# A perceiver block on one core: where the attentions of the tokens keep their row sums and largest scores in PSUM

## The chip, the core and the metric

The kernel runs on one core of a Trainium2 chip. The metric is the device time of one execution in microseconds (us); the median of several runs is compared. The profile shown here is one further execution, taken with the hardware profiler. TensorE is called PE (its weight loads PEld), VectorE DVE, ScalarE ACT, GpSimd POOL and SyncE SP.

## The reference

Twelve blocks are added to x one after another, x being 2 sequences of 256 tokens with 256 features: four times a cross attention, a self attention and a feed-forward part. The edit touches the self attentions of the second and the fourth layer (L1 and L3), both with 16 heads of 16 features. That of L1, shortened to what matters:

```python
scale = jnp.asarray(k, x.dtype) ** 0.25
q = (jnp.einsum('btk,ok->bto', x, Wq) / scale).reshape(b, t, H, hd)
kk = (jnp.einsum('btk,ok->bto', x, Wk) / scale).reshape(b, t, H, hd)
v = jnp.einsum('btk,ok->bto', x, Wv).reshape(b, t, H, hd)
dot = jnp.einsum('bthd,bshd->bhts', q, kk)
att = jax.nn.softmax(dot, axis=-1)
out = jnp.einsum('bhts,bshd->bthd', att, v).reshape(b, t, k)
return jnp.einsum('btk,ok->bto', out, Wu) + bu
```

That of L3 is the same with biases and with a band: a query sees the keys that are at most 128 tokens away. In front of each attention is a layer norm.

## The kernel before

Both attentions are the class SmallAttention (L1336), called by small_attention (L1322). The 16 heads lie in four chunks c of four heads, each head in 32 of the 128 partitions; 2 sequences b by 4 chunks are the 8 units (b, c), u = 0 to 7, of `UNITS` (L1342). A unit has 256 queries and 256 keys for four heads.

For one unit the work is a chain:

- **first_scores** (L1451): PE makes the scores with the queries in the partitions (`both`, matmuls at L1430, groups s<-sa_k,sa_q of two pairs of heads; L3 adds the band with matmuls at L1438), and DVE takes the largest of each row, negated, from each pair (L1455), into sa_top.
- **shift_queries** (L1463): PE transposes the largest scores into a bank of PSUM, top_ps (L1467), and DVE adds them to a spare row of the queries (L1468), so that the second scores come out with the largest already taken off.
- **scores** (L1470): PE makes the scores again with the keys in the partitions (L1430, s<-sa_q,sa_k, in L3 with L1438), and ACT takes the exponential of each pair (L1475), into p.
- **weigh** (L1478): PE multiplies p with the values (L1485) into attn_acc; one more column of the values is 1, so that the sums of the weights come out beside the result. ACT copies the accumulator into a (L1493).
- **Net.inverses** (L195): PE turns the rows with the sums into columns (sums, matmul at L180), and DVE takes their reciprocals (L201).
- **Net.to_heads** and **normalize** (L204, L1495): PE spreads the reciprocals over each head's partitions (den, L209) and DVE multiplies a by them into sa_oT (L1500).

The loop `attend` (L1405) runs as a pipeline of n + 4 = 12 steps. In step i it calls inverses for unit i-4, shift_queries for i-1, first_scores for i, weigh for i-3, scores for i-1 and normalize for i-4. PE, DVE and ACT run in the order in which the program issues (`manual_schedule`, L1325), so this order is the order of each engine's queue; no planner is in it. No DMA is issued in the loop.

All of PSUM's eight banks are in use in the loop (L1330): `banks(mm=1, sc=3, acc=1)`, that is three pairs of banks for scores (tag sc), one bank for the accumulator (acc), one for everything else (mm). sums, top_ps and den are each a whole new bank with the tag mm, so each of the three waits until the reader of the one before it is done. The queries of the next unit use the same three sc pairs in turn: a step takes four of them.

The same inverses and to_heads also serve the cross attentions of L0 and L1 (the class ContextAttention, L780), with banks of their own.

Of the kernel before, what the change touches and what calls it, by code (L numbers as in the profile page):

```python
# [28 lines left out]
S = 256  # L29
# [41 lines left out]
class Net:  # L71
# [120 lines left out]
            nc.vector.tensor_tensor(rest, of, part, ALU.subtract)  # L192
        nc.vector.tensor_copy(outs[:, 2, ..., :n], rest)

    def inverses(self, a):  # L195

        ps = self.mm("sums")
        for qt in range(2):
            self.matmuls(ps[:, qt * NG : (qt + 1) * NG], [(a[:, qt * P : (qt + 1) * P], self.den)])
        r = self.small.tile([P, 2, NG], F32, tag="inverses", name="inverses", bufs=2)  # L200
        self.nc.vector.reciprocal(r, ps[:, : 2 * NG].rearrange("p (q g) -> p q g", g=NG))  # L201
        return r

    def to_heads(self, r):  # L204

        ps = self.mm("den")
        for qt in range(2):
            for g in range(NG):
                self.nc.tensor.matmul(  # L209
                    ps[g * HP : (g + 1) * HP, qt * P : (qt + 1) * P],  # L210
                    lhsT=r[:, qt, g : g + 1].to_broadcast([P, HP]),
                    rhs=self.ident,
                    start=True,
                    stop=True,
                )
        return ps[:, :S]
# [105 lines left out]
    def self_attention(self, work, qT, kT, v_of, oT, mask=None, causal=False, gates=None, before=None, negated=None):  # L322
# [98 lines left out]
        with self.tc.manual_schedule(engines=by_program):  # L421
            if before is not None:
                before(0)
            for n in range(len(items) + 6):
                if before is not None and n % 4 == 1 and n // 4 + 1 < qT.shape[1]:
                    before(n // 4 + 1)
                if n < len(items):
                    scores(n)
                if 0 <= n - 1 < len(items):
                    share(n - 1)  # L430
                if 0 <= n - 3 < len(items):
                    transpose(n - 3)
                if 0 <= n - 5 < len(items) and items[n - 5][2] == 1:
                    weigh(n - 5)
# [153 lines left out]
def run(steps, n=None):  # L588

    for _ in steps if n is None else zip(range(n), steps):  # L590
        pass


class Focus:
# [28 lines left out]
    def weigh(self, y, total, factor):  # L623


        nc = self.nc
        top, norm = (self.net.sm(NT, name=n, tag=n) for n in ("f_top", "f_norm"))
        nc.scalar.activation(y, y, AF.Ln, bias=self.eps)

        ready = self.net.sm(1, name="ready", tag="ready")  # L630
        nc.scalar.activation(ready, self.eps, AF.Exp)
        nc.gpsimd.tensor_scalar(y, y, self.power[:, 0:1], 1.0, ALU.mult, ALU.mult)
        yield
        nc.vector.tensor_reduce(top, y, AX.X, ALU.max, negate=True)
        yield
        for t in range(NT):
            nc.scalar.activation(
                y[:, t, :], y[:, t, :], AF.Exp, bias=top[:, t : t + 1], accum_out=norm[:, t : t + 1]
            )
            if t % 2:  # L640
                yield
        nc.vector.tensor_tensor(factor, total[:, 0, :], total[:, 1, :], ALU.add)
        nc.vector.tensor_scalar(factor, factor, 1.0 / D, 1e-6, ALU.mult, ALU.add)
        nc.vector.reciprocal(norm, norm)
        nc.vector.tensor_tensor(factor, factor, norm, ALU.mult)
# [134 lines left out]
class ContextAttention:  # L780
# [195 lines left out]
    def attend(self, vpool, ppool, fpool):  # L976
        net, nc, PER, LAG = self.net, self.nc, self.PER, self.LAG
        focus = net.focus
        self.vpool, self.ppool = vpool, ppool
        for _ in range(4):  # L980
            self.load_values_ctx()
        focus.start(self.layer, fpool)
        fills = self.plan()
        n = len(self.UNITS)

        ready = net.sm(1, name="ready", tag="ready")
        nc.scalar.activation(ready, net.eps5, AF.Exp)
        rankings = {}
        for g in range((n + 1) * PER + LAG + 2):
            second = g - PER - LAG  # L990
            if g < n * PER:
                self.first_scores(g // PER, g % PER)
            run(self.beginning)
            run(fills.get(g, ()))
            for kc in self.rankings.get(g, ()):
                if kc not in rankings:
                    y, _, factor = focus.chunks[kc]
                    rankings[kc] = focus.sparsify(fpool, y, factor)
                run(rankings[kc], 1)
            if 0 <= second < n * PER:  # L1000
                self.scores(second // PER, second % PER)
            focus.magnitudes_of_taken()
            if 0 <= second - 1 < n * PER:
                self.weigh((second - 1) // PER, (second - 1) % PER)
            if g in self.done:
                self.inverses = net.inverses(self.weighed)
                if self.done[g] == n - 1:
                    run(self.normalize(n - 1))
            for kc in self.weighings.get(g, ()):
                run(focus.weighing[kc], 1)  # L1010
# [73 lines left out]
    def shift_queries(self, u):  # L1084

        nc = self.nc
        ps = self.net.mm("top_ps")
        for qt in range(2):
            nc.tensor.transpose(ps[:, qt * P : (qt + 1) * P], self.tops[qt], self.net.ident)
        yield  # L1090
        nc.vector.tensor_tensor(self.q[u], self.q[u], ps[:, :S], ALU.add)

    def normalize(self, u):

        nc, out = self.nc, self.q[u]
        nc.vector.tensor_tensor(out, self.weighed, self.net.to_heads(self.inverses), ALU.mult)
        if self.v_bias is not None:
            c = self.UNITS[u][1]
            nc.vector.tensor_scalar_add(out, out, self.v_bias[:, c : c + 1])
        yield  # L1100
# [235 lines left out]
class SmallAttention:  # L1336
# [66 lines left out]
            made = []  # L1403

    def attend(self):  # L1405
        n = len(self.UNITS)
        for i in range(n + 4):
            if 0 <= i - 4 < n:
                self.inverses = self.net.inverses(self.weighed[i - 4])
            if 0 <= i - 1 < n:  # L1410
                self.shift_queries(i - 1)
            if i < n:
                self.first_scores(i)
            if 0 <= i - 3 < n:
                self.weigh(i - 3)
            if 0 <= i - 1 < n:
                self.scores(i - 1)
            if 0 <= i - 4 < n:
                self.normalize(i - 4)

    def both(self, name, rows_of, columns_of):

# [37 lines left out]
                negate=True,  # L1460
            )

    def shift_queries(self, u):  # L1463

        ps = self.net.mm("top_ps")
        for qt in range(2):
            self.nc.tensor.transpose(ps[:, qt * P : (qt + 1) * P], self.tops[u % 2][:, qt, :], self.net.ident)  # L1467
        self.nc.vector.tensor_tensor(self.q[u], self.q[u], ps[:, :S], ALU.add)  # L1468
# [9 lines left out]
    def weigh(self, u):  # L1478
        nc = self.nc
        b, c = self.UNITS[u]  # L1480
        acc, ps = self.net.acc("attn_acc"), self.weights.pop(u)
        for kt in range(2):
            for i in range(NG):
                at = (c * NG + i) * VH
                nc.tensor.matmul(  # L1485
                    acc[i * HP : (i + 1) * HP, :S],
                    lhsT=self.v[:, b * 2 + kt, at : at + HP],
                    rhs=ps[i // 2][:, i % 2, kt * S : (kt + 1) * S],
                    start=kt == 0,
                    stop=kt == 1,  # L1490
                )
        self.weighed[u] = self.work.tile([P, S], F32, name="a", tag="a", bufs=3)
        nc.scalar.copy(self.weighed[u], acc[:, :S])  # L1493

    def normalize(self, u):  # L1495

        nc, a = self.nc, self.weighed.pop(u)
        b, c = self.UNITS[u]
        den = self.net.to_heads(self.inverses)
        nc.vector.tensor_tensor(self.oT[:, c, b * S : (b + 1) * S], a, den, ALU.mult)  # L1500


# [825 lines left out]
```

## Time and profile before

| what | us |
|---|---|
| median of the 3 runs | 2512.33 |
| runs | 2512.18, 2512.33, 2951.45 |
| the profiled execution | 2515.34 |
| its span, first to last instruction | 2513.4 |
| L1's attention, from its first scores to its last product | 1644.7 to 1704.3 |
| L3's attention, the same | 2174.5 to 2243.9 |

The mean granted clock of TensorE over the span is 0.958 of full speed. In groups by line, the operations of the loop (both attentions together) are: maxima L1455, 32 of 1221 ns; exponentials L1475, 32 of 1021 ns; L1468 and L1500, 16 each of 421 ns; the copies L1493, 16 of 372 ns. The reciprocals L201 are 32 of 207 ns, of which the cross attentions have half.

In a row of the timeline, the first number is the start in us from the span's start, the second the time from the first start to the last end of a merged group of like instructions; a bracket at the end is the time that the engine was idle before, with what ended it. A matmul of 32-bit numbers, transposes aside, shows as two instructions. A row of the stretches gives the length, then for PE, PEld, DVE, ACT and POOL the busy us with the number of instructions, then TensorE's granted clock, the busy share of the DMA engines and what they moved in GB/s. A row of the waits gives who waited for whom: us in total, times, longest.

### The profile page before, as it was taken

How to read it: one execution, taken by the hardware profiler on the slowest of the kernel's cores; microseconds unless marked ns; L12 is line 12 of the kernel's file. 1: busy time of each engine (PE TensorE's matmuls, PEld its weight loads, DVE VectorE, ACT ScalarE, POOL GpSimd, SP SyncE). 2: the span in 40 equal slices, each digit the busy share in tenths (PEclk: the TensorE clock that was granted, in tenths of full speed). 3: DMA queues.
4: the chain of work that ended last, by engine and by line, in shares of the span. 5: the costliest groups of instructions: out<-in, count | busy, mean ns of one | idle time of the engine just before them, and what ended most of it. 6: DMA issues, size and time to landing. Idle time of an engine off the chain costs nothing.

```text
span 2513.4 us, 42846 instructions
## 1 busy us (share of the span) xinstructions
PE 2336.0 (93%) x17142; PEld 1252.9 (50%) x17142; DVE 1549.4 (62%) x2719; ACT 1093.2 (43%) x1917; POOL 333.2 (13%) x505
## 2 busy tenths in 40 slices
PE   7999999999999689999999999989999996889998
PEld 3455455544544364554454544554448453455454
DVE  4878888788736757877878778443241354334343
ACT  2456555555615333555555565531131252123232
POOL 3000001000024602000010000000011031002120
PEclk9999999999989799999999999989999997798989
DMA  5432232132010133322222220201232100100100
GB/s 185 138 105 86 88 96 94 52 111 64 10 38 35 48 103 108 101 91 90 90 94 86 77 98 28 83 14 43 96 100 93 43 18 14 34 21 12 58 12 21
DMA packets 97798, 174.42 MB, mean 69 GB/s; under 512 B 15120, under 2 KB 63888, under 8 KB 96704
## 3 DMA queue, kind: packets, MB, share of 16 engines
q1 hardware_dynamic: 97600, 171.68, 21.1%
q8 instruction: 136, 2.23, 0.4%
q14 instruction: 62, 0.51, 0.1%
HBM read 154.25 MB, written 0.59 MB: 62 GB/s over the span
## 4 chain that ended last, share of the span: by engine, by line
PE 57%; DVE 6%; ACT 2%; issue 1%; POOL 0%; DMA 0%; SPq 0%; ACTq 0%; DVEq 0%; POOLq 0%
PE s L1113 6%; PE s L1137 5%; PE proj L180 5%; PE attn_acc L1161 5%; PE v_ps L180 4%; PE expert L180 2%; PE k_ps L1034 2%; PE s L180 2%; PE c_acc L1753 2%; PE s L1430 2%; PE ffn_ps L180 2%; DVE mx L1121 2%; PE scores L342 1%; PE f_ps L180 1%; PE kc_sum L180 1%; PE qk_ps L180 1%
## 5 line engine op out<-in xcount | busy, mean ns | idle before, releaser
L1121 DVE TENSOR_REDUCE mx<-s 128x2 f32<-128x1024 f32 x512 | 603.2, 1221 | 224.6 <-PE s L1113 221.8
L1147 ACT ACTIVATE p<-s 128x1024 f32<-128x1024 f32 x512 | 496.0, 1021 | 255.8 <-PE s L1137 253.8
L1137 PE MATMUL s<-xa_q,xa_k 32*128 32x256 f32 x4096 | 342.3, 403 | 26.0 <-DVE mx L1121 23.0
L1113 PE MATMUL s<-xa_k,xa_q 32*128 32x512 f32 x2048 | 338.7, 642 | 7.0 <-ACT p L1147 2.3
L1137 PEld LDWEIGHTS s<-xa_q,xa_k 32*128 32x128 f32 x4096 | 212.7, 184 | 167.5 <-issue 92.6
L1161 PE MATMUL attn_acc<-p,xv 128*32 128x256 f32 x4096 | 276.2, 386 | 0.7 <-ACT p L1147 0.7
L1113 PEld LDWEIGHTS s<-xa_k,xa_q 32*128 32x128 f32 x2048 | 111.4, 183 | 124.7 <-issue 60.6
L667 DVE TENSOR_TENSOR ge<-fy 128x960 bf16<-128x960 f32 (+14 forms) x240 | 169.5, 706 | 6.5
L1161 PEld LDWEIGHTS attn_acc<-p,xv 128*32 128x32 f32 x4096 | 107.4, 109 | 131.4 <-issue 84.4
L621 POOL TENSOR_TENSOR fy<-fy,low 128x256 f32<-128x256 f32 x64 | 46.4, 725 | 881.3 <-ACT fy L620 881.1
L669 DVE TENSOR_TENSOR rank<-rank,ge 128x960 bf16<-128x960 bf16 (+14 forms) x240 | 104.2, 434 | 6.0
L671 DVE TENSOR_TENSOR rank<-rank,ge 128x960 bf16<-128x960 bf16 (+14 forms) x240 | 100.8, 420 | 2.6
L387 POOL TENSOR_SCALAR p<-p,r 128x128 f32<-128x128 f32 (+1 forms) x192 | 82.6, 442 | 127.0 <-DVE r L383 72.4
L1081 ACT COPY xv<-v_ps 128x512 f32<-128x512 f32 x64 | 37.6, 587 | 135.7 <-PE v_ps L180 135.7
L368 ACT ACTIVATE p<-p,top 128x256 f32<-128x256 f32 (+1 forms) x128 | 57.1, 447 | 66.6 <-DVE top L356 65.3
L180 PE MATMUL f_ps<-f_wk,f_ctx 128*128 128x256 f32 x256 | 68.9, 400 | 0.6 <-DMA f_ctx<-in_ctxT 0.6
L1034 PE MATMUL k_ps<-ctx_k,w_L0x_wq 128*64 128x512 f32 x256 | 66.0, 612 | 3.2 <-DMA ctx_k<-in_ctxT 2.9
L180 PE MATMUL v_ps<-w_L0x_wv,ctx_v 128*128 128x256 f32 x256 | 65.6, 400 | 0.8 <-ACT k_dense L1047 0.8
L180 PEld LDWEIGHTS f_ps<-f_wk,f_ctx 128*128 128x128 f32 x256 | 44.4, 189 | 43.3 <-issue 26.5
L1753 PE MATMUL c_acc<-pT,ctx_n 128*128 128x256 f32 x256 | 62.0, 387 | 4.2 <-ACT pT L1726 3.0
L180 PE MATMUL kc_sum<-f_tok,fy 128*128 128x257 f32 x256 | 64.2, 393 | 0.0
L180 PE MATMUL v_ps<-w_L1x_wv,ctx_v 128*128 128x256 f32 x256 | 63.8, 392 | 0.0
(478 smaller groups left out, 3366.8 us busy)
## 6 DMA issues: line engine op xcount, KB each, us to landing
ctx_k<-in_ctxT SPq DMA_DIRECT2D x128, 512.0 KB
ctx_v<-in_ctxT SPq DMA_DIRECT2D x64, 256.0 KB
xa_k<-k_dense SPq DMA_DIRECT2D x512, 32.0 KB
f_ctx<-in_ctxT SPq DMA_DIRECT2D x32, 256.0 KB
f_tok<-in_ctx SPq DMA_DIRECT2D x16, 512.0 KB
ctxT<-in_ctxT SPq DMA_DIRECT2D x16, 512.0 KB
ctx_n<-in_ctx SPq DMA_DIRECT2D x16, 512.0 KB
xa_k<-key_masks SPq DMA_DIRECT2D x128, 8.0 KB
```

The lines of the kernel that those rows point to most:

```text
L180: self.nc.tensor.matmul(out, lhsT=lhsT, rhs=rhs, start=i == 0, stop=i == len(pairs) - 1)
L387: nc.gpsimd.tensor_scalar(p[:, j, :nk], p[:, j, :nk], r[:, j : j + 1], 1.0, ALU.mult, ALU.mult)
L667: nc.vector.tensor_tensor(ge[:, :, :n], w[:, :, :n], w[:, :, P - n :], ALU.is_ge)
L669: nc.vector.tensor_tensor(rank[:, :, P - n :], rank[:, :, P - n :], ge[:, :, :n], ALU.add)
L671: nc.vector.tensor_tensor(rank[:, :, :n], rank[:, :, :n], ge[:, :, :n], ALU.subtract)
L1034: nc.tensor.matmul(ps[i * HR : (i + 1) * HR, :], lhsT=self.wk[:, d, c * HR : (c + 1) * HR], rhs=ctx[:, d, :], start=d == 0, stop=d == ND - 1,)
L1113: nc.tensor.matmul(pairs[i // 2][:, i % 2, :], lhsT=self.q[u][rows, qt * P : (qt + 1) * P], rhs=k[rows, :], start=True, stop=True,)
L1121: nc.vector.tensor_reduce(mx[:, qt, 2 * i : 2 * i + 2, kc], sc, AX.X, ALU.max)
L1137: nc.tensor.matmul(pairs[i // 2][:, i % 2, kk * S : (kk + 1) * S], lhsT=k[rows, at], rhs=self.q[u][rows, :], start=True, stop=True,)
L1147: nc.scalar.activation(p, sc, AF.Exp, scale=DH**-0.5)
L1161: nc.tensor.matmul(self.acc[i * HP : (i + 1) * HP, :S], lhsT=v[:, 2 * k2 + kk, at : at + HP], rhs=ps[i // 2][:, i % 2, kk * S : (kk + 1) * S],
L1753: nc.tensor.matmul(accs[m], lhsT=of[:, (k + i) % (KC // P), m * P : (m + 1) * P], rhs=pT[:, i, :], start=k + i == 0, stop=k + i == KT - 1,)
```

## The change

The call of normalize (den and L1500) moves ahead of the second scores. The call of inverses moves to the end of the step and takes unit i-3, the one that has just been weighed, so that den of the next step uses a reciprocal of the step before. The sums go into the upper half of the accumulator's bank (columns 256 and up; weigh uses the lower half). top_ps and den of a step are the two halves of one bank with the tag mm, named aux. inverses and to_heads can be given a place in PSUM; without one they do as before.

```diff
-    def inverses(self, a):
+    def inverses(self, a, ps=None):
-        ps = self.mm("sums")
+        ps = self.mm("sums") if ps is None else ps
...
-    def to_heads(self, r):
+    def to_heads(self, r, ps=None):
-        ps = self.mm("den")
+        ps = self.mm("den") if ps is None else ps
...
     def attend(self):
         n = len(self.UNITS)
         for i in range(n + 4):
-            if 0 <= i - 4 < n:
-                self.inverses = self.net.inverses(self.weighed[i - 4])
+            aux = self.net.mm("aux") if 0 <= i - 1 else None
             if 0 <= i - 1 < n:
-                self.shift_queries(i - 1)
+                self.shift_queries(i - 1, aux[:, S:])
             if i < n:
                 self.first_scores(i)
             if 0 <= i - 3 < n:
                 self.weigh(i - 3)
+            if 0 <= i - 4 < n:
+                self.normalize(i - 4, aux[:, :S])
             if 0 <= i - 1 < n:
                 self.scores(i - 1)
-            if 0 <= i - 4 < n:
-                self.normalize(i - 4)
+            if 0 <= i - 3 < n:
+                self.inverses = self.net.inverses(self.weighed[i - 3], self.acc[:, S:])
...
-    def shift_queries(self, u):
-        ps = self.net.mm("top_ps")
+    def shift_queries(self, u, ps):
...
-        acc, ps = self.net.acc("attn_acc"), self.weights.pop(u)
+        self.acc = acc = self.net.acc("attn_acc")
+        ps = self.weights.pop(u)
...
-    def normalize(self, u):
+    def normalize(self, u, ps):
...
-        den = self.net.to_heads(self.inverses)
+        den = self.net.to_heads(self.inverses, ps)
```

## The prediction

> **What bounds the kernel now.** I read first the page's shares and its clock row, then the table of stretches over the two attentions that the edit touches, then who waited for whom in one of them, and last one step in the order of time.
>
> From the page, the line of busy shares and the row of granted clock (40 slices of 62.8 us):
>
> ```profile
> PE 2336.0 (93%) x17142; PEld 1252.9 (50%) x17142; DVE 1549.4 (62%) x2719; ACT 1093.2 (43%) x1917; POOL 333.2 (13%) x505
> ...
> PEclk9999999999989799999999999989999997798989
> ```
>
> TensorE sets the time of the kernel as a whole. The attentions with heads of 16 lie in slices 27 and 35 and are small, so what can be won has to be read there. The table of stretches (busy us and count of PE, PEld, DVE, ACT, POOL; then clock, DMA share, GB/s), for L1's attention up to its steady part, its steady steps 4 to 7, its tail, and the same three for L3's:
>
> ```profile
> 1644.70:1666.00 21.30, 17.17 (x136) 9.90 (x135) 12.05 (x14) 6.25 (x7) 0.00 (x0) 0.68 0.12 38
> 1666.00:1690.50 24.50, 20.49 (x285) 13.00 (x281) 13.63 (x20) 10.81 (x14) 0.00 (x0) 1.00 0.01 1
> 1690.50:1704.30 13.80, 11.09 (x148) 6.98 (x149) 2.92 (x9) 3.42 (x6) 0.42 (x1) 0.88 0.01 1
> ...
> 2174.50:2203.20 28.70, 24.63 (x163) 14.26 (x163) 12.76 (x16) 6.25 (x7) 0.00 (x0) 0.64 0.12 38
> 2203.20:2231.10 27.90, 23.93 (x315) 14.97 (x312) 13.62 (x20) 10.31 (x14) 0.00 (x0) 1.00 0.01 2
> 2231.10:2243.90 12.80, 10.04 (x152) 6.67 (x153) 2.93 (x9) 3.92 (x6) 1.98 (x5) 1.00 0.01 1
> ```
>
> The steady parts run at clock 1.00 with PE at 84 to 86% and no engine full: they are bound by a chain of waits. PE's waits between 1666 and 1704.3 us:
>
> ```profile
> PE sums L180 <- DVE sa_oT L1500: 4.9, 7, 0.7
> PE top_ps L1467 <- DVE inverses L201: 1.5, 5, 0.3
> PE den L209 <- DVE inverses L201: 0.3, 1, 0.3
> ```
>
> The reason is the one bank with the tag mm: sums, top_ps and den take it in turn, each after the reader of the one before. One step in the timeline (start, duration, engine):
>
> ```profile
> 1678.25 0.58 PE L180 MATMUL sums<-den,a 128*128 128x4 f32 x4 [0.71 <-DVE sa_oT L1500]
> 1678.86 0.21 DVE L201 RECIPROCAL inverses<-sums 128x8 f32<-128x8 f32 x1 [0.76 <-PE sums L180]
> ...
> 1679.13 0.44 PE L1467 MATMUL top_ps<-ident,sa_top 128*128 128x128 f32 x2 [0.30 <-DVE inverses L201]
> ...
> 1679.50 1.15 PE L1430 MATMUL s<-sa_k,sa_q 32*128 32x256 f32 x16
> ...
> 1680.57 1.07 PE L1485 MATMUL attn_acc<-p,sa_v 128*32 128x256 f32 x16
> ...
> 1680.68 2.36 DVE L1455 TENSOR_REDUCE sa_top<-s 128x4 f32<-128x1024 f32 x2 [0.65 <-PE s L1430]
> ...
> 1681.57 1.52 PE L1430 MATMUL s<-sa_q,sa_k 32*128 32x256 f32 x16
> ...
> 1683.02 0.64 PE L209 MATMUL den<-ident,inverses 128*32 128x128 f32 x16
> 1683.80 0.42 DVE L1500 TENSOR_TENSOR sa_oT<-a,den 128x256 f32<-128x256 f32 x1 [0.77 <-PE den L209]
> ```
>
> The next sums start at 1684.37: a step is 6.12 us.
>
> **The change, part by part.** No arithmetic, DMA or instruction of an engine is added or removed; nothing passes SP's or POOL's queue. I work with intervals from the start of one PE group to that of the next, which contain the handover. Before, in L1: sums to top_ps 0.88, to first scores 0.37, to weigh 1.07, to second scores 1.00, to den 1.45, to the next sums 1.35: together 6.12.
>
> *The sums go to the end of the step, into the free half of the accumulator's bank.* They need a, which ACT copies from 1681.71 to 1682.08, a microsecond before the second scores end: no wait. Their reciprocal is used a pass later. So top_ps follows the sums directly: 0.51, the interval from sums to the next group where nothing is waited for (1696.79 to 1697.30). That is 0.37 saved. A new wait: the next weigh takes the only accumulator bank and so stands behind that reciprocal. It comes 0.51 + 0.37 + 1.07 = 1.95 us after the sums' start, the reciprocal ends after 0.82: hidden while top_ps and the first scores lie between, and if that cover goes it costs 0.88 - 0.51 = 0.37 (it does in the tail).
>
> *den moves ahead of the second scores.* Its reciprocal is then a pass old. den to the next group is 0.57 (2242.69 to 2243.26, den to proj), in place of 1.35 with the wait for L1500: 0.78 saved. And the second scores come 0.57 later after the first, so that their second pair no longer waits for the first maximum (first scores start + 1.18 + 1.22): they take 1.07, as in L3's tail, in place of 1.45: 0.38 saved.
>
> *top_ps takes the upper half of a bank that den's half shares.* The new wait: top_ps behind the previous L1500, which stands in DVE's queue behind two maxima. From the start of top_ps: 0.37, then 1.18 until the maxima start, 2.36, L1500 0.42, handover 0.14: 4.47. Behind top_ps hang L1468, the second scores, everything on PE.
>
> *The score banks* are unchanged (three pairs), but the first scores' second pair needs the first exponential of the step before. That starts 1.18 after the second scores (1664.91 to 1666.09), takes 0.97, handover 0.11: 2.26; PE would come there at 1.07 + 0.51 + 0.37 + 0.27 = 2.22. I count 0.05.
>
> PE's own sum for a step in L1 is 0.51 + 0.37 + 1.07 + 1.00 + 0.57 + 1.07 + 0.05 = **4.64**, above DVE's loop of 4.47, so PE sets it. Four steps (4 to 7) took 1690.49 - 1665.99 = 24.50 and will take 18.56: 5.94 saved. In L3 the mask's matmuls add 0.54 and 0.45 after the two scores: 0.51 + 0.36 + 1.08 + 0.54 + 1.00 + 0.57 + 1.07 + 0.45 = 5.58; four steps took 2231.15 - 2203.26 = 27.89 and will take 22.32: 5.57 saved.
>
> Step 8 has no first scores: in L3 0.51 + 0.36 + 1.00 + 0.57 + 1.07 + 0.45 = 3.96 in place of 5.22, 1.26 saved; in L1 3.51 in place of 6.30, 2.79 saved, of which about half is that before it ran at a slow clock (weigh 1.78 and scores 2.06 in place of 1.07 and 1.15). Steps 9 and 10: weigh waits for the reciprocal (0.88), then a's copy 1.14 + 0.37 later and 0.11 more for the sums: 2.50 in place of 2.72, 0.22 saved, four times 0.88. Step 11 is as before. Steps 0 to 3 have no den and their sums stay where they were in time: nothing saved.
>
> Sum: 5.94 + 5.57 + 1.26 + 2.79 + 0.88 = **16.4 us**. The profiled execution took 2515.34 (span 2513.4 and 1.9 around it), 3.0 above the median of the runs, 2512.33. So 2515.3 - 16.4 = 2498.9 for such an execution, and **2496.0** beside the median, which is my forecast. The sum's bounds: if the handovers that no trace shows (L1500 to top_ps, exponential to first scores) each cost 0.3 a step, 8 steps give back 5; the least is no gain on top.
>
> **Two rules of the Trainium skill against this.** The clock row of the tail in L1 shows 0.88, that in L3 1.00, with the same instructions. "TensorE: Matmul & The Clock Gate", section "A second HAM failure mode: psum-queue depth-cycling", says that a PE which micro-idles between groups while it cycles through banks can fall back to half clock again and again. By the rule L1's tail stays slow: step 8 then wins 1.2 as in L3 instead of 2.79, sum 14.8. By the row of the steady part (1.00 at 84% busy) a denser stretch has no cause to fall. I follow the row, as PE's idle time shrinks. "PSUM — Partial Sum Buffer", section "PSUM bank collisions raise a hardware error", asks that engines be kept apart by bank and quadrant, not by address: halves of one bank then don't free each other. The row: by the intervals above each such pair is in order anyhow (den comes 2.4 us after top_ps and 1.0 after L1468 ended; sums need a's copy). By the rule only weigh behind the reciprocal remains, 0.37 in each of four tail steps, which the sum holds; without it the sum would be up to 1.5 more.
>
> **Rivals.**
> *A wait in the place of the one removed:* top_ps behind L1500. For it: only 0.17 us between 4.64 and 4.47, and DVE runs two maxima, L1500 and the reciprocal in strict order. Against it: in L3 the loop has 0.6 to spare. If DVE falls behind by about 1 us a step, half the gain of the eight steps and a part of the tails go: 2504.
> *The change does nothing*, because the halves are guarded so that den waits for the same pass as before: then 2512, at most 1 away. Against: the reader of each is a pass old.
> *Bigger:* stages behind keep a faster clock by chance of phase (0.5 to 0.9 in several 20-us stretches after 2060): up to 8 us more, 2488.
> *Slower than before:* the granted clock stays at a half through the attentions, as in their first steps (0.68 and 0.64). The groups then take 2.08/1.15 = 1.8 times: steps of 8.3 and 10.1, which over four steps each is 8.7 and 12.4 above before, and 1.9 in the tail: 2535. It decides from the point where about 42% of the steps are slow (16.4 of 16.4 + 23). Against: before, with more idle time, the steady parts were at 1.00.
>
> **How the numbers follow.** Forecast 0.72 (own range 2490 to 2502: 5 given back, or some us of clock phase either way), a wait in its place 0.13 (2502 to 2508), nothing 0.05, slower 0.05, bigger 0.05. The range 2488 to 2506 holds the first and the bigger ones nearly whole and most of the second. A measurement tells about 2% from no change, 50 us. The two attentions' touched parts last 79 us in all, and no case worked out reaches that: faster 0.01, same 0.97, slower 0.02.
>
> **What would show it.** Steps of 4.6 and 5.6 us in the two attentions; PE's waits for L1500 and L201 gone but for the tail, where weigh waits for L201 about 0.3; second scores of 1.15; den directly behind weigh; tail clock in L1 at 1.00. Wrong would be: top_ps waiting for L1500 in each step, first scores waiting for p, or a clock under 0.9 in the steady parts.

## The result and the profile after

| | before | after |
|---|---|---|
| median, us (20 runs each) | 2520.47 | 2502.34 |
| profiled execution, us | 2515.34 | 2499.71 |
| its span | 2513.4 | 2497.7 |

The ratio is that of the fast executions alone (one of before, at 2951.45, is left out): 0.9936, with a 95% interval of 0.9919 to 0.9954, so about 16 us of 2520, or 12 to 20 (forecast: 16.4 of 2512, a ratio of 0.9935). That the two ratios agree to 0.0001 is luck: the interval alone is 9 us wide. The median of after, 2502.34, is 6.3 above the forecast of 2496.0 and just outside of the inner range of 2490 to 2502, inside the outer one of 2488 to 2506. The median of before had risen by 8 us with more runs; an experiment below puts that spread in the stages that the edit does not touch.

The lines of after lie up to 4 further down: L201, L1430, L1455, L1467, L1475, L1485 and L1500 of before are L202, L1434, L1459, L1470, L1478, L1489 and L1504.

The busy shares of the page of after hardly move, which is as it must be where only waits go:

```profile
PE 2333.2 (93%) x17142; PEld 1252.7 (50%) x17142; DVE 1545.5 (62%) x2719; ACT 1093.5 (44%) x1917; POOL 334.0 (13%) x505
```

The stretches of after, cut where those of before were: steady steps 4 to 7 and tail in L1, then the same two in L3 (length; busy us of PE, PEld, DVE, ACT, POOL; clock; DMA):

```profile
1660.80:1680.10 19.30, 19.30 (x285) 13.06 (x281) 13.24 (x20) 9.24 (x12) 0.00 (x0) 1.00 0.01 2
1680.10:1690.80 10.70, 9.35 (x152) 6.30 (x149) 2.94 (x9) 4.99 (x7) 0.42 (x1) 1.00 0.01 2
...
2191.50:2214.20 22.70, 22.70 (x314) 15.57 (x313) 13.24 (x20) 9.24 (x12) 0.00 (x0) 1.00 0.01 2
2214.20:2225.20 11.00, 9.66 (x154) 6.57 (x153) 2.93 (x9) 4.89 (x7) 1.98 (x5) 1.00 0.02 4
```

The same instructions took 24.5 and 27.9 us in the steady parts; now PE is shown busy from end to end, at 19.3 and 22.7 (the wait that is left lies inside a group of matmuls and counts as busy, see below). PE's waits in L1's attention of after, 1660.8 to 1690.8 us:

```profile
PE attn_acc L1489 <- DVE inverses L202: 0.7, 2, 0.4
PE aux L210 <- DVE inverses L202: 0.4, 1, 0.4
```

The 4.9 us behind L1500 are gone. Only the tail waits for the reciprocal. One step of after in the timeline (sums are now written attn_acc<-den,a, after the bank that they share; top_ps and den are aux):

```profile
1670.45 0.61 PE L180 MATMUL attn_acc<-den,a 128*128 128x4 f32 x4
1670.61 1.94 ACT L1478 ACTIVATE p<-s 128x1024 f32<-128x1024 f32 x2 [1.17 <-PE s L1434]
...
1670.92 0.42 PE L1470 MATMUL aux<-ident,sa_top 128*128 128x128 f32 x2
...
1671.26 1.56 PE L1434 MATMUL s<-sa_k,sa_q 32*128 32x256 f32 x16
...
1672.47 2.36 DVE L1459 TENSOR_REDUCE sa_top<-s 128x4 f32<-128x1024 f32 x2 [0.68 <-PE s L1434]
...
1672.75 1.07 PE L1489 MATMUL attn_acc<-p,sa_v 128*32 128x256 f32 x16
...
1673.64 0.62 PE L210 MATMUL aux<-ident,inverses 128*32 128x128 f32 x16
...
1674.19 1.15 PE L1434 MATMUL s<-sa_q,sa_k 32*128 32x256 f32 x16
1674.74 0.41 DVE L1504 TENSOR_TENSOR sa_oT<-a,aux 128x256 f32<-128x256 f32 x1
```

The next sums start at 1675.27: a step is 4.82 us in place of 6.12 (5.69 in place of 6.99 in L3). Two things are to be seen besides the gap that closed. The second scores are 1.15 long in place of 1.52. The first scores have grown from 1.15 to 1.56, in L3 from 1.15 to 1.54, and no wait stands beside them: a wait inside a merged group shows only in its length. L3, before and after:

```profile
2218.41 1.15 PE L1430 MATMUL s<-sa_k,sa_q 32*128 32x256 f32 x16
...
2203.56 1.54 PE L1434 MATMUL s<-sa_k,sa_q 32*128 32x256 f32 x16
```

Since the rest of the kernel varies by several us, the kernels are compared below by the steps and by the *touched stretch*, from the start of the first sums to the first matmul of the projection. It fell from 37.70 to 29.36 us in L1 and from 40.00 to 33.09 in L3, together by 15.25. The span fell by 15.7: 5.1 us earlier at L1's attention already, and 4.7 given back behind the two attentions, in stages that the edit does not touch.

### The profile page after: what moved, and what is told of

The parts are those of the page before. It is cut to its first block, busy times and chain, and to the rows that moved or that the text cites. A ratio compares the mean times of both kernels' runs of the same rounds, so it can differ in the third digit from the quotient of the medians.

```text
span 2497.7 us, 42812 instructions
## 1 busy us (share of the span) xinstructions
PE 2333.2 (93%) x17142; PEld 1252.7 (50%) x17142; DVE 1545.5 (62%) x2719; ACT 1093.5 (44%) x1917; POOL 334.0 (13%) x505
## 4 chain that ended last, share of the span: by engine, by line
PE 57%; DVE 5%; ACT 2%; POOL 1%; issue 1%; DMA 0%; ACTq 0%; SPq 0%; DVEq 0%; POOLq 0%
PE s L1114 6%; PE proj L180 5%; PE s L1138 5%; PE attn_acc L1162 5%; PE v_ps L180 4%; PE expert L180 2%; PE k_ps L1035 2%; PE s L180 2%; PE c_acc L1757 2%; PE s L1434 2%; PE ffn_ps L180 2%; DVE mx L1122 2%; PE scores L343 1%; PE kq_ps L180 1%; PE f_ps L180 1%; PE kc_sum L180 1%
```

## The experiments

Sums only, den only and more banks are edits of the kernel before, the others of the change. All kernels, in us; ratio to the kernel before, with its interval where it was timed more than once:

| kernel | step L1 | step L3 | stretch L1 | stretch L3 | ratio |
|---|---|---|---|---|---|
| before | 6.12 | 6.99 | 37.70 | 40.00 | |
| before again | 6.12 | 6.99 | 37.70 | 40.01 | 1.0011 (0.9992 to 1.0031) |
| the change | 4.82 | 5.69 | 29.36 | 33.09 | 0.9936 (0.9919 to 0.9954) |
| sums only | 5.07 | 5.95 | 30.44 | 34.71 | 0.9920 (0.9894 to 0.9945) |
| den only | 5.26 | 5.76 | 31.74 | 33.99 | 0.9926 (0.9896 to 0.9955) |
| sums in mm | 5.26 | 5.76 | 31.75 | 33.99 | |
| turns, not halves | 4.82 | 5.69 | 29.37 | 33.09 | |
| den first | 5.49 | 6.17 | 33.43 | 36.37 | 0.9955 (0.9926 to 0.9983) |
| half exponentials | 4.40 | 5.29 | 27.76 | 31.57 | |
| weigh split | 5.07 | 5.74 | 30.41 | 33.36 | 0.9955 (0.9937 to 0.9974) |
| more banks, old order | 6.28 | 7.45 | 35.82 | 40.36 | |

A step is the time from the sums of one unit to those of the next, in the steady part and from the second on. The intervals of the variants' ratios overlap, so a difference of 1 to 3 us between them is read from the steps and stretches alone. The steps agree within 0.03 us from one to the next and, in the one kernel that was traced twice, within 0.01 between the traces.

### The kernel before, again

No edit.

> The kernel before, unchanged, against itself. My theory: a ratio of 1.000 within the interval; the steps of the two attentions again 6.12 and 6.99 us, the stretch from the first sums to the projection 37.7 less about 1.5 in L1 (in the first profile that tail ran at a slow clock, which I take for chance: step 8 5.0 in place of 6.3) and 40.0 in L3; the stages that the edit does not touch differ by some us. Rival (the slow clock of L1's tail belongs to the old order): step 8 again about 6.3 with the clock at 0.9.

The steps and both stretches came out the same within 0.01 us, while the spans of the two traces differ by 10.8 us (2524.2 against 2513.4). So the noise lies outside of the touched stretches. My expectation that the slow clock in L1's tail was chance **fell**: step 8 took 6.30 again (sums at 1698.27 and 1704.57), with the same fall of the clock. The tail's stretch in this second trace:

```profile
1698.30:1711.80 13.50, 10.78 (x147) 6.86 (x148) 2.64 (x9) 3.41 (x6) 0.42 (x1) 0.87 0.00 1
```

### Only the sums move

```diff
-            if 0 <= i - 4 < n:
-                self.inverses = self.net.inverses(self.weighed[i - 4])
...
             if 0 <= i - 4 < n:
                 self.normalize(i - 4, self.net.mm("den"))
+            if 0 <= i - 3 < n:
+                self.inverses = self.net.inverses(self.weighed[i - 3], self.acc[:, S:])
```

> Only the sums move: to the end of the step, into the free half of the accumulator's bank; top_ps and den stay turns of the one mm bank and den stays behind the second scores. My theory (each part removes the wait that it stands in front of, and the rest is the order on PE): sums no longer wait, but top_ps now waits for L1500: steps in L1 of 0.36 + 1.07 + 1.00 + 1.45 + 1.35 = 5.23 us in place of 6.12, in L3 6.11 in place of 6.99; second scores still 1.5 long; in all about 8 us saved, ratio 0.997. Rival (the shared bank under the sums was the whole matter, where den stands is worth nothing): steps of 4.8 and 5.7 and 16 us saved.

Steps of 5.07 and 5.95, stretches 12.55 us shorter together: the mechanism as expected, 0.16 better a step (den to top_ps takes 1.19 in place of the 1.35 that I took over from den to the sums) and better in the tail. top_ps waits behind L1503 while the sums fill most of that time:

```profile
1672.18 0.64 PE L210 MATMUL den<-ident,inverses 128*32 128x128 f32 x16
...
1672.75 0.61 PE L180 MATMUL attn_acc<-den,a 128*128 128x4 f32 x4
...
1672.89 0.42 DVE L1503 TENSOR_TENSOR sa_oT<-a,den 128x256 f32<-128x256 f32 x1 [0.70 <-PE den L210]
...
1673.37 0.44 PE L1469 MATMUL top_ps<-ident,sa_top 128*128 128x128 f32 x2
```

The rival, that the sums' bank was the whole matter, falls: 0.25 a step is missing. This part alone brings 82% of the change's 15.25 us. Which of its two sides does it, the sums' place in the order or their own bank, no run with den left late takes apart.

### Only den moves

```diff
+            if 0 <= i - 4 < n:
+                self.normalize(i - 4)
             if 0 <= i - 1 < n:
                 self.scores(i - 1)
-            if 0 <= i - 4 < n:
-                self.normalize(i - 4)
```

> Only den and its product move ahead of the second scores; sums, top_ps and den stay turns of the one mm bank. My theory: the sums of the next step wait for L1500, which stands behind two maxima (first scores + 1.18 + 2.36 + 0.42 + 0.14 = 4.10), so L1's step is 4.10 + 0.88 + 0.36 = 5.34; in L3 PE comes there later (4.59) than L1500 (4.43), so nothing waits and the step is 5.83, nearly the whole gain without any change of banks. Second scores 1.15 long in both. In all about 10 us saved. Rival (the halves of banks bring the gain): 6.1 and 7.0, nothing saved.

Steps of 5.26 and 5.76 (expected 5.34 and 5.83), stretches 11.97 us shorter, with no change of banks at all: moving one call brings 78% of the gain. What remains in L1 is the wait of the sums for L1500, now behind two maxima, and of top_ps for the reciprocal:

```profile
1674.05 0.58 PE L180 MATMUL sums<-den,a 128*128 128x4 f32 x4 [0.35 <-DVE sa_oT L1500]
```

It was 0.71 there. The two parts alone add to 24.5 us, the change has 15.25: they shorten the same loop, and either one takes most of it.

### The sums at the end, but in mm's turn

```diff
-                self.inverses = self.net.inverses(self.weighed[i - 3], self.acc[:, S:])
+                self.inverses = self.net.inverses(self.weighed[i - 3])
```

> The whole change, but the sums at the end of the step take a turn of the one mm bank in place of the accumulator's free half. My theory: they then wait for L1504, behind two maxima, and top_ps for the reciprocal, as when only den moved: steps of 5.26 in L1 and 5.76 in L3 (measured there). Rival (with the sums at the end of the step and den early, the order alone brings the gain): 4.82 and 5.69.

5.26 and 5.76, the same as with den alone. So once den is early, putting the sums a pass ahead of their use is worth nothing by itself; the 0.44 in L1 and 0.07 in L3 come from their own place.

### top_ps and den in turns, not in halves

```diff
-            aux = self.net.mm("aux") if 0 <= i - 1 else None
...
-                self.shift_queries(i - 1, aux[:, S:])
+                self.shift_queries(i - 1, self.net.mm("top_ps"))
...
-                self.normalize(i - 4, aux[:, :S])
+                self.normalize(i - 4, self.net.mm("den"))
```

> The whole change, but top_ps and den are turns of the one mm bank again, not halves of a shared one; the sums stay in the accumulator's half. With den ahead of the first scores it waited 0.5 us for the reader of the other half of its bank, so halves of a bank are kept apart like turns. My theory: the same steps as the change, 4.82 and 5.69. Rival (the halves free something): den waits, steps of 5.1 and 5.9.

4.82 and 5.69 again, stretches the same to 0.01 us. The shared bank for top_ps and den does nothing; of the "halves" only that of the sums counts.

### den ahead of the first scores

```diff
+            if 0 <= i - 4 < n:
+                self.normalize(i - 4, aux[:, :S])
             if i < n:
                 self.first_scores(i)
             if 0 <= i - 3 < n:
                 self.weigh(i - 3)
-            if 0 <= i - 4 < n:
-                self.normalize(i - 4, aux[:, :S])
```

> The whole change, with den and its product moved on, ahead of the first scores. In the changed kernel the first scores last 1.5 us in place of 1.15. My theory: their second pair waits there for the first exponential of the step before, 0.4 a step that my sum had at 0.05. With den in between PE comes later: first scores 1.15 again, steps of 0.47 + 0.35 + 0.06 + 0.55 + 1.07 + 1.00 + 1.24 = 4.74 in L1 (second scores' second pair again waits 0.17 for the first maximum, den 0.06 for the reciprocal) in place of 4.82, 5.58 in L3 in place of 5.69. About 1 us better than the change. Rival (first scores are stretched by something else, such as two readers and a writer in PSUM at once): they stay at 1.5, steps of 4.9 and 5.8.

The first scores came back to 1.15 as expected, but the steps are 5.49 and 6.17: 0.7 and 0.5 worse than the change, where I had expected 0.1 better. Two costs that I had at 0.06 and 0.17 did it in L1. den waits for the reader of the *other* half of its bank (top_ps to den 0.93 in place of 0.35), and the second scores wait for the first maximum again (1.45 in place of 1.07):

```profile
1661.40 0.64 PE L210 MATMUL aux<-ident,inverses 128*32 128x128 f32 x16 [0.51 <-DVE sa_q L1471]
...
1664.05 1.52 PE L1434 MATMUL s<-sa_q,sa_k 32*128 32x256 f32 x16
```

In the change den comes 2.7 us after top_ps, when that reader is long done.

### Exponentials half as long

```diff
-            self.nc.scalar.activation(p, sc, AF.Exp, scale=self.scale)
+            self.nc.scalar.activation(p[:, :, :S], sc[:, :, :S], AF.Exp, scale=self.scale)
...
-                    rhs=ps[i // 2][:, i % 2, kt * S : (kt + 1) * S],
+                    rhs=ps[i // 2][:, i % 2, :S],
```

> The whole change, but only the first 256 of 512 columns of each score tile get an exponential, and the product with the values uses them twice (so the weights of the second half of the keys are left out). Exponentials of about 0.55 us in place of 0.97. My theory: first scores 1.15; L1's step falls to the next bound, top_ps behind L1504, 4.45 to 4.5 (PE alone 0.47 + 0.35 + 1.07 + 0.89 + 0.55 + 1.07 = 4.40), L3's to 5.3. Rival (first scores are not waiting for the exponentials): 4.82 and 5.69 as in the change.

The kernel leaves out half of the exponentials and with them the weights of half of the keys; PE's matmuls are as many and as large as in the change. First scores 1.15, steps of 4.40 and 5.29:

```profile
1668.90 1.09 ACT L1478 ACTIVATE p<-s 128x512 f32<-128x512 f32 x2 [1.17 <-PE s L1434]
...
1669.55 1.15 PE L1434 MATMUL s<-sa_k,sa_q 32*128 32x256 f32 x16
```

So the growth of the first scores in the change is the wait for the exponential. 4.40 is also exactly PE's own sum (0.47 + 0.35 + 1.07 + 0.89 + 0.55 + 1.07), so DVE's loop, which I had put at 4.45 to 4.5, is not above it.

### The product with the values in two parts

```diff
+            if 0 <= i - 3 < n:
+                self.weigh(i - 3, 0)
             if i < n:
                 self.first_scores(i)
             if 0 <= i - 3 < n:
-                self.weigh(i - 3)
+                self.weigh(i - 3, 1)
```

> The whole change, and the product with the values is cut in two: its first half (keys 0 to 127) ahead of the first scores, its second behind them. My theory: what is left of waiting in the change is the first scores' second pair behind the exponential of the step before, 0.4 a step. With 0.5 more work of PE ahead of it that wait goes (first scores 1.15), while the first product now comes 0.88 after the sums, behind the reciprocal (0.06 late in L1, 0.16 in L3), and the second scores come nearer to the first maximum (1.07 + 0.5 + 0.55 + 0.14 = 2.26 against 2.50, 0.24 late in L1, nothing in L3): 4.40 + 0.06 + 0.24 = 4.70 in L1 and 5.69 - 0.36 + 0.16 = 5.49 in L3, some 1.3 us in all better than the change. Rival (a cut product loses as much in its handovers as it wins): 4.8 and 5.7 or more.

5.07 and 5.74: the wait for the exponential went (first scores 1.15), but the second scores wait for the first maximum (1.45) and the first half of the product takes 0.57 to the next group:

```profile
1671.33 0.64 PE L1492 MATMUL attn_acc<-p,sa_v 128*32 128x256 f32 x8
...
1671.90 1.15 PE L1436 MATMUL s<-sa_k,sa_q 32*128 32x256 f32 x16
...
1673.98 1.51 PE L1436 MATMUL s<-sa_q,sa_k 32*128 32x256 f32 x16
```

The rival was right. As I read it, PE's work of a step is too little to hide both waits: what is moved ahead of the first scores is missing ahead of the second.

### More banks in the old order

```diff
-            with net.banks(mm=1, sc=3, acc=1):
+            with net.banks(mm=2, sc=2, acc=2):
```

> The kernel before in its old order, with the banks dealt differently: two for mm, two pairs for scores, two for accumulators, in place of one, three, one. My theory: sums and top_ps no longer wait for each other, but the second scores wait for both maxima and the first scores for both exponentials: a loop of 3.65 + 0.8 + 0.2 + 1.94 less 0.27, about 6.3 to 6.5 us in L1, 6.9 to 7.3 in L3; nothing won. Rival (a second bank is all that was missing): 4.9 and 5.7.

6.28 and 7.45 (0.15 above what I had for L3). In the steps PE's matmuls no longer wait for L1500 or the reciprocal; the second scores wait for the maxima in their place, in L3 the first scores for the exponentials too:

```profile
1680.04 0.70 PE L1430 MATMUL s<-sa_q,sa_k 32*128 32x256 f32 x4 [0.18 <-DVE sa_top L1455]
1681.17 1.13 PE L1430 MATMUL s<-sa_q,sa_k 32*128 32x256 f32 x12 [0.43 <-DVE sa_top L1455]
```

The stretch of L1 is 1.9 shorter all the same: step 8 takes 3.70 in place of 6.30, for in this trace the slow clock is not there but in the first full step (7.61), and steps 9 and 10 take 2.1 in place of 2.7. All eight banks were in use before, so the second banks for mm and acc had to come from the scores; what they would bring without that, no run shows.

## Why the prediction was right, and where its terms were off

The mechanism held step by step: sums to top_ps 0.47 (0.51 predicted), weigh to den 0.89 (1.00), den to second scores 0.55 (0.57), second scores 1.07 (1.07), no wait for L1504, sums' new place free. Measured against the sum:

| saved, us | predicted | measured |
|---|---|---|
| four steps, L1 | 5.94 | 5.30 |
| four steps, L3 | 5.57 | 5.20 |
| step 8, L1 and L3 | 2.79 + 1.26 | 2.82 + 1.40 |
| steps 9 and 10, both | 0.88 | 0.70 |
| step 11, both | 0 | -0.17 |
| sum | 16.4 | 15.25 |

**The mis-sized term** is "I count 0.05" for the first scores behind the exponential: it is about 0.4 in each of eight steps, in L3 too, where I had nothing. The small part of it is that the exponential ends 0.1 later than I had it: it starts 1.24 after the second scores and lasts 1.02, the length of one, not 0.97, half of a merged group whose two overlap. The large part is that I let the second pair of the first scores start 0.27 into the group. The two pairs are issued in turns of two matmuls, so the second needs its bank almost at once: in the single records of before's trace its first matmul starts 0.01 us after the group's (1679.50 and 1679.51). In the change it starts 0.43 after it (1671.26 and 1671.69), 0.05 after the first exponential's end at 1671.64. The other intervals came out shorter than mine and paid about two thirds of it back; without that luck the eight steps would have saved some 2 us less.

**The tail in L1** came out as forecast, for the clock of after's tail is 1.00. My reason, that a denser stretch has no cause to fall, is not shown. The slow clock of before is no chance, as I took it to be ahead of the second run of that kernel. The fall is there in both traces of it, at the same place of the program though the second runs 7.8 us later, and it lasts 3.4 us at 0.50. It is in none of the eight traces in which den or the sums moved; with more banks in the old order it came in the first full step instead. So far as these traces go, about half of step 8's gain in L1 comes from the clock and belongs to the change (an estimate: 6.30 before, against the 4.77 that L3's step 8 takes without the 0.45 of its mask). Which of the two that I weighed was right is read from step 8 (2.82, where the rule had 1.2) and not from the sum, as 15.25 lies nearer to the 14.8 of the rule. That rule of the Trainium skill ("TensorE: Matmul & The Clock Gate", section "A second HAM failure mode: psum-queue depth-cycling", on a PE that micro-idles between groups) fits what the *old* order did there; that the micro-idling is the cause is not shown. What in the old order sets it off at step 8 of L1, and not in L3, is open: no run takes the order's idle time apart from its kind of work.

**The rule on banks** ("PSUM — Partial Sum Buffer", section "PSUM bank collisions raise a hardware error"): I wrote that each pair of accesses is in order anyhow, with only weigh behind the reciprocal left. In the change this held (the two waits of 0.35 to 0.4 in each tail). "Den first" shows that den does wait for the reader of the other half of its bank, 0.5 us a step as soon as the two halves are used in close order; it is the program that waits there, and whether the chip needs it no run shows. "Turns, not halves" shows that in the change the halves of aux bring nothing.

**The rivals.** A wait in the place of the one removed did come, though not from L1500, where I looked for it, but from the exponential, and it took 3.1 us (eight first scores, 0.33 to 0.41 each). "First scores waiting for p" stood among my own signs of being wrong: it came in every one of these steps, and they are 4.82 and 5.69 in place of the 4.6 and 5.6 that I had named. That nothing happens, or the slow clock throughout, is refuted by the steps and by the clock of 1.00. The untouched stages moved by some us in either direction, as allowed for.

## What to carry to other kernels

Where several small uses take turns in one bank, first try the order: move a use so that other work of the engine lies between it and the next one, which waits for its reader. Here moving one call, with no bank touched, brought 78% of the gain (moving the sums into a free half of a bank, without it, 82%; the two overlap). Halves of a bank help only where each half's reader is done before the other half's writer comes. When a wait is removed from a loop, work out every buffer that the faster loop will ask for earlier, at the first instruction of a group that needs it and not at the middle, and look for the new wait in the length of a merged group.

## What the hardware showed that I had not expected

TensorE's granted clock falls to 0.50 for 3.4 us, right behind a stretch in which PE is 84% busy at 1.00, and does so at the same place in both traces of the same program. From the kernel before, three neighbouring stretches around it:

```profile
1690.50:1692.00 1.50, 1.20 (x11) 0.84 (x15) 0.36 (x2) 0.37 (x1) 0.00 (x0) 0.98 0.00 0
1692.00:1693.40 1.40, 1.40 (x16) 0.43 (x8) 0.26 (x1) 0.00 (x0) 0.00 (x0) 0.50 0.05 12
1693.40:1695.40 2.00, 2.00 (x20) 1.22 (x16) 0.00 (x0) 0.37 (x1) 0.00 (x0) 0.51 0.00 0
```

PE is shown fully busy in the slow stretch, because its groups take up to 1.8 times as long there (weigh 1.78 in place of 1.07, second scores 2.06 in place of 1.15): a full row of busy time with a low clock beside it is a loss, not a gain.
